# A mixture-of-experts stage: the shared expert's way down, one batch behind its way up

## The chip, the core and the metric

The kernel runs on one core of a Trainium2 chip. A core has TensorE (matrix products; PE in the profile), VectorE (DVE), ScalarE (ACT), GpSimd (POOL) and SyncE (SP, which here only issues DMAs). Each engine works through its own queue in order. Engines wait for each other, and for DMAs, through semaphores. Tiles lie in SBUF, 128 partitions wide; the results of TensorE go to tiles in PSUM, here each in a buffer of its own that is called a bank below.

The metric is the device time of one execution, in microseconds. The kernel before takes 3576.08 us (median of three runs, 3575.98 to 3579.71).

## The reference

The program is two layers, each a cross attention and a feed-forward part, over x of 4 batches of 512 tokens of 512 values. The change lies in the first layer's feed-forward part, a mixture of experts:

```python
scores = softmax(xf @ gate_w)                    # 8 experts
_, sel = top_k(scores + expert_bias, 2)
top_scores = take_along_axis(scores, sel, axis=1)
...
routed_in = xf[token_idx] * top_scores_sorted[:, None]
h = silu(ragged_dot(routed_in, w1, counts)) * ragged_dot(routed_in, w3, counts)
routed_out = ragged_dot(h, w2, counts)
out = silu(xf @ sw1) * (xf @ sw3) @ sw2          # the shared expert
out = out.at[token_idx].add(routed_out)
```

`xf` is the layer-normed x, and `out` is scaled by a gate and added to x. The hidden width is 448. Every token goes through the shared expert (`sw1`, `sw3`, `sw2`), and through two of eight routed ones.

## The kernel before

The program runs through four stages: int8 cross attention, this mixture of experts (`moe`), a second cross attention and a second feed-forward part. All arithmetic named here is f32; an f32 matmul or transpose of the program is two rows in the profile.

**Order.** The kernel is written with the Tile framework. It traces the calls, and a scheduler then decides in which order each engine's queue takes them, by the order of the calls and by when it takes the inputs to be ready; it also inserts all waits. A call that is wrapped by `Ordered` (lines 559 to 567) is pinned: it stays behind the call that was traced just before it on the same engine. In `moe` before the change nothing up to the slot loop is pinned. Tiles of one tag share a fixed number of buffers, and are given out in the order of the calls.

**First part of `moe`** (lines 660 to 679). For each batch b of four: a layernorm on VectorE (`k.layernorm`) makes `xn[b]` of four token tiles; sixteen transposes on TensorE (L670), four to each PSUM tile `pt` of the pool `ps_m` (two banks), which `k.evac` copies to `xT[b]`, by turns on VectorE (L120) and ScalarE (L122); then sixteen matmuls with the gate's weights (L675) into `pg`, also of `ps_m`, copied to the logits.

**Shared expert**, `shared(b)` (lines 683 to 705). The way up has four chunks m of 112 hidden columns. A chunk has four matmuls into `pu` and four into `pw` (L691; pool `ps_h`, four banks), a SiLU on ScalarE (L695) into `h`, and a product of `h` with `pw` on VectorE (L696). The way down has four token tiles t. A tile has four matmuls, one for each chunk of `h` (L700, pool `ps_o`, two banks), and a sum into the residual x on VectorE (L705). `shared(b)` does the four chunks, then the four tiles; it is called for all batches after the routing (L821).

**Routing** (lines 716 to 802). VectorE works out each token's two experts; two matmuls with the 0/1 matrix `both` count tokens (L750, L751); VectorE turns the counts into a row number of each token and choice, and into the owner of each of 39 slots of 128 rows.

**Scatters** (lines 807 to 819). For each of 16 token tiles and both choices, VectorE scales a tile of `xn` into `row` (tag `m_row`, four buffers, L811), and POOL issues an indirect DMA that writes it to `slots_in` in DRAM (L815).

**Slots** (lines 825 to 938). `load(s)` and `load_down(s)` bring the weights of slot s from its owner expert (L833: 1792 KB, L855: 896 KB, SP's queue) into `w13[s % 2]` and `w2[s % 2]`; `w13[1]` and `w2[1]` hold the shared expert's weights until slot 1. `load_rows(s)` (L837, ScalarE's queue) reads the slot's rows; it waits for all scatters. `turn_in(s)` transposes them (L861), `up(s)` and `down(s)` are the expert (L870, L888). The loop over s also calls, a few at a time, the steps of `split` (each loads a piece of a later stage's weights into one of two `raw` buffers, scales and centres it on VectorE at L1115 to L1137, casts it on ScalarE at L1141, subtracts on POOL at L1142, and stores it at L1143) and of `ternary` (weight sums at L1897 over pieces `t_raw`, which take the buffers of `xT` when these come free; codes at L1920). The scheduler takes such steps forward when it holds an engine to be free: the trace has them from 629 us on, in the midst of the shared expert.

After the loop, from L947 on, everything is pinned.

Of the kernel before, what the change touches and what calls it, by code (L numbers as in the profile page):

```python
# [11 lines left out]
F32 = mybir.dt.float32  # L12
# [6 lines left out]
ALU = mybir.AluOpType  # L19
# [578 lines left out]
def moe(k, split, codes8, scratch, ffn):  # L598
# [12 lines left out]
    with ExitStack() as ctx:  # L611
# [50 lines left out]
        for b in range(B):  # L662
            xn.append(p6.tile([P, TB, D], F32, tag="m_big", name=f"m_xn{b}"))
            xT.append(codes8.place(b, F32, f"m_xT{b}"))
        for b in range(B):
            k.layernorm([(xn[b][:, t, :], k.x[:, b * TB + t, :]) for t in range(TB)])
            for c in range(KC):
                pt = ps_m.tile([P, S], F32, tag="ps_m")
                for t in range(TB):
                    nc.tensor.transpose(pt[:, ts(t, P)], xn[b][:, t, ts(c, P)], k.ident)  # L670
                k.evac(xT[b][:, c, :], pt)
            pg = ps_m.tile([P, TB, E], F32, tag="ps_m")
            for t in range(TB):
                for c in range(KC):
                    nc.tensor.matmul(  # L675
                        pg[:, t, :], lhsT=xT[b][:, c, ts(t, P)], rhs=gw[:, c, :],
                        start=(c == 0), stop=(c == KC - 1),
                    )
            k.evac(lg[:, ts(b, TB), :], pg)

        silus = []

        def shared(b):

            h = p6.tile([HC, NHC, S], F32, tag="m_big", name=f"m_h{b}")
            for m in range(NHC):
                pu = ps_h.tile([HC, S], F32, tag="ps_h")
                pw = ps_h.tile([HC, S], F32, tag="ps_h")
                for half, pp in enumerate((pu, pw)):
                    for c in range(KC):  # L690
                        nc.tensor.matmul(  # L691
                            pp, lhsT=w13[1][:, c, half, ts(m, HC)], rhs=xT[b][:, c, :],
                            start=(c == 0), stop=(c == KC - 1),
                        )
                silus.append(nc.scalar.activation(h[:, m, :], pu, AF.Silu).ins)  # L695
                nc.vector.tensor_tensor(h[:, m, :], h[:, m, :], pw, ALU.mult)  # L696
            for t in range(TB):
                po = ps_o.tile([P, D], F32, tag="ps_o")
                for m in range(NHC):
                    nc.tensor.matmul(  # L700
                        po, lhsT=h[:, m, ts(t, P)], rhs=w2[1][:, m, :],
                        start=(m == 0), stop=(m == NHC - 1),
                    )
                xt = k.x[:, b * TB + t, :]
                nc.vector.scalar_tensor_tensor(xt, po, k.tg[:, 2:3], xt, ALU.mult, ALU.add)  # L705

        def bc(col):
            return col[:, :, None].to_broadcast([P, NT, E])
# [38 lines left out]


        pt = ps_m.tile([P, 2, NT, E], F32, tag="ps_m", name="r_counts")
        nc.tensor.matmul(pt[:, 0], lhsT=k.ones, rhs=both, start=True, stop=True)  # L750
        nc.tensor.matmul(pt[:, 1], lhsT=before, rhs=both, start=True, stop=True)  # L751
        nc.vector.tensor_copy(csum[0][:, 8:, :], pt[:, 0])
        src = 0
        for d in (1, 2, 4, 8):
# [63 lines left out]
                tc.declare_no_dep(scatters[-1], group="scatter", reason="rows are distinct")  # L818
                tc.add_to_no_dep_group("scatter", scatters[-1])

        for b in range(B):  # L821
            shared(b)
        got = {}

        def load(s):


            e = got["e", s] = nc.values_load(
                owners[:, s : s + 1], engines=(mybir.EngineType.SP,), min_val=0, max_val=E - 1,
                skip_runtime_bounds_check_because="it is at most E - 1 by construction",  # L830
            )
            got["new", s] = None if s < 2 else e != got["e", s - 2]
            nc.sync.dma_start(w13[s % 2], a["w13"][e], cond=got["new", s])  # L833
# [20 lines left out]
        def load_down(s):  # L854
            nc.sync.dma_start(w2[s % 2], a["w2"][got["e", s]], cond=got["new", s])  # L855

        def turn_in(s):
            work = got["work", s]
            pt = ps_m.tile([P, KC, P], F32, tag="ps_m")
            for c in range(KC):  # L860
                nc.tensor.transpose(pt[:, c, :], work[:, 0, ts(c, P)], k.ident)  # L861
            k.evac(work[:, 1, :].rearrange("p (c t) -> p c t", c=KC), pt)

        def up(s):
            work, w = got["work", s], w13[s % 2]
# [42 lines left out]
        ternary = ffn.weights(codes8, ps_o)  # L908
        for s in range(4):
            load_rows(s)  # L910
        for s in range(2):
            load(s)
            load_down(s)
        turn_in(0)
        up(0)
        turn_in(1)
        for s in range(SLOTS):
            if s + 1 < SLOTS:
# [1113 lines left out]
```

## Time and profile before

| what | value |
|---|---|
| median of three runs | 3576.08 us |
| the profiled execution, its own time | 3574.1 us |
| its span, first to last instruction | 3572.4 us |
| mean granted TensorE clock | 0.97 |
| `moe` from the first transpose to slot 0's first matmul | 629.88 to 870.42 us |
| shared expert's ways up, L691 | 256 rows, 642.8 to 845.6 us (starts) |
| shared expert's ways down, L700 | 128 rows, 689.2 to 868.7 us (starts) |
| slot loop's ways up, L870 | 312 rows for each of pu and pw, 870.4 to 1306.3 us (starts) |
| product on VectorE, L696 | 16 of 0.68 us |
| sum on VectorE, L705 | 16 of 0.74 us |
| row scaling, L811 / scatter, L815 | 32 of 0.485 us / 32 of 0.963 us |

A time in the table is read from the span's start. In lists of waits, a row says which instruction waited for which, the sum in us, how often, and the longest. In a timeline, a row gives start, length, engine, line, operation, output<-input, shape and count, and in brackets the idle time before it with what ended it. The granted clock is the share of TensorE's full clock that the chip allowed it.

### The profile page before, as it was taken

Reading aid. Unit: us, or ns where it says so; the run is one execution under the profiler, and the core shown is the slowest. Engines: PE = TensorE matmul, PEld = TensorE weight load, DVE = VectorE, ACT = ScalarE, POOL = GpSimd, SP = SyncE. Lnnn points to the kernel's source line nnn. Section 1 sums busy time; section 2 is a strip of 40 time slices with the busy share of each in tenths; the row PEclk is TensorE's granted clock in tenths of the full one; section 3 lists DMA queues with packets and bytes.
Section 4 is the critical chain, followed back from the end, with each engine's and each line's share of the span. In section 5 each row is a group of like instructions: output and inputs, shape, how many; then the busy total and the mean of one; then the engine's idle time right before and its main releaser. Section 6 shows DMA issues by size and latency. Waiting matters only on the chain.

```text
span 3572.4 us, 47015 instructions
## 1 busy us (share of the span) xinstructions
PE 3333.4 (93%) x15536; PEld 2190.3 (61%) x15552; DVE 2172.4 (61%) x4580; ACT 1544.1 (43%) x4456; POOL 1355.3 (38%) x1526
## 2 busy tenths in 40 slices
PE   6988987889999889989999999999999999999997
PEld 3544544534554444447777777776777777777775
DVE  6676767543133336525558766678766687676657
ACT  2544545111211223345554455554555554555543
POOL 1000000341000134624446654557545466544443
PEclk8999999899999999989999999999999999999998
DMA  5534441476354673552323233223332332333211
GB/s 183 156 98 130 121 101 41 167 254 234 104 198 151 225 257 128 177 174 72 115 98 107 101 115 110 95 99 108 109 125 92 118 107 77 128 105 111 83 60 36
DMA packets 223026, 452.86 MB, mean 127 GB/s; under 512 B 21440, under 2 KB 80320, under 8 KB 220224
## 3 DMA queue, kind: packets, MB, share of 16 engines
q1 hardware_dynamic: 206432, 412.62, 35.2%
q10 hardware_dynamic: 11232, 20.45, 1.7%
q0 software_dynamic: 5120, 16.78, 1.4%
q8 instruction: 125, 2.05, 0.2%
q14 instruction: 117, 0.96, 0.1%
HBM read 420.87 MB, written 116.98 MB: 151 GB/s over the span
## 4 chain that ended last, share of the span: by engine, by line
PE 73%; DVE 13%; DMA 4%; ACT 4%; POOL 3%; issue 3%; SPq 0%; DVEq 0%; POOLq 0%; ACTq 0%
PE ps_w L567 10%; PE pss L567 10%; PE ps_p L567 9%; PE ps_o L567 9%; PE ps_t L567 7%; PE m_pk L567 5%; PE po L888 3%; PE pu L870 3%; PE pw L870 3%; PE po L468 3%; PE pt L460 3%; DVE f_y L567 2%; PE pss L438 2%; PE pk L403 2%; PE pv L373 2%
## 5 line engine op out<-in xcount | busy, mean ns | idle before, releaser
L567 PEld LDWEIGHTS ps_w<-g_pT,g_v 128*128 128x128 f32 x2048 | 388.8, 191 | 299.7 <-issue 223.1
L567 ACT ACTIVATE g_p<-pss,nm 128x512 f32<-128x512 f32 x512 | 350.9, 685 | 479.7 <-DVE nm L567 436.4
L567 PE MATMUL ps_w<-g_pT,g_v 128*128 128x256 f32 x2048 | 530.4, 382 | 24.1 <-DVE f_y L567 13.7
L567 PE MATMUL pss<-g_kT,g_qT 128*128 128x512 f32 x1024 | 524.1, 594 | 0.9 <-ACT g_p L567 0.9
L567 POOL TENSOR_SCALAR g_p<-g_p,rs 128x512 f32<-128x512 f32 x512 | 368.4, 721 | 382.1 <-DVE rs L567 370.6
L567 DVE TENSOR_REDUCE nm<-pss 128x1 f32<-128x512 f32 x512 | 350.9, 685 | 102.7 <-PE pss L567 101.7
L567 PE MATMUL ps_t<-ident,g_p 128*128 128x128 f32 x2048 | 307.5, 273 | 0.0
L1142 POOL TENSOR_TENSOR hl<-raw,hl 128x512 fp32r<-128x512 f32 x80 | 102.0, 1282 | 519.2 <-ACT hl L1141 503.1
L567 POOL TENSOR_TENSOR g_rstd<-ss,neghalf 128x4 f32<-128x4 f32 (+1 forms) x192 | 185.0, 964 | 297.5 <-ACT ss L567 297.3
L567 PE MATMUL ps_p<-g_wq,g_xq 128*128 128x512 f32 x1024 | 282.3, 417 | 5.3 <-DMA g_wq<-s_q 4.9
L567 PE MATMUL ps_o<-g_wp,g_cq 128*128 128x512 f32 x1024 | 287.0, 423 | 0.0
L567 DVE COPY g_pT<-ps_t 128x512 f32<-128x512 f32 x244 | 167.1, 685 | 165.8 <-PE ps_t L567 165.4
L567 POOL TENSOR_TENSOR f_t<-f_y,f_c 128x512 f32<-128x512 bf16 (+1 forms) x180 | 206.6, 1148 | 155.4 <-DVE f_c L567 87.1
L567 PEld LDWEIGHTS ps_t<-ident,g_p 128*128 128x128 f32 x2048 | 243.8, 141 | 26.3 <-POOL g_p L567 1.1
L567 ACT COPY g_pT<-ps_t 128x512 f32<-128x512 f32 x268 | 156.1, 583 | 233.4 <-PE ps_t L567 233.4
L446 ACT ACTIVATE p<-pss,nm 128x512 f32<-128x512 f32 x256 | 175.3, 690 | 135.9 <-DVE nm L443 134.5
L567 PE MATMUL m_pk<-m_wx,m_ctxT 128*128 128x512 f32 x512 | 230.0, 592 | 0.0
L567 PEld LDWEIGHTS ps_o<-g_wp,g_cq 128*128 128x128 f32 x1024 | 196.7, 192 | 41.4
L567 PEld LDWEIGHTS ps_p<-g_wq,g_xq 128*128 128x128 f32 x1024 | 191.4, 190 | 48.9 <-issue 7.1
L443 DVE TENSOR_REDUCE nm<-pss 128x1 f32<-128x512 f32 x256 | 173.2, 687 | 70.7 <-PE pss L438 69.3
L567 ACT ACTIVATE junk<-ps_p 128x128 f32<-128x128 f32 x640 | 177.1, 277 | 68.5 <-PE ps_p L567 54.2
L567 DVE RECIPROCAL rs<-g_sm 128x1 f32<-128x1 f32 x512 | 82.5, 161 | 203.3 <-ACT g_p L567 201.4
(317 smaller groups left out, 6025.4 us busy)
## 6 DMA issues: line engine op xcount, KB each, us to landing
m_w<-in_w_dram SPq DMA_DIRECT2D x39, 1792.0 KB
g_wp<-s_proj SPq DMA_DIRECT2D x128, 512.0 KB
m_w<-in_w_dram SPq DMA_DIRECT2D x39, 896.0 KB
g_wq<-s_q SPq DMA_DIRECT2D x128, 256.0 KB
g_wq<-s_qx SPq DMA_DIRECT2D x128, 256.0 KB
st_k<-dhl_k SPq DMA_DIRECT2D x64, 256.0 KB
st_q<-dhl_q SPq DMA_DIRECT2D x64, 256.0 KB
s_proj<-hl SPq DMA_DIRECT2D x32, 512.0 KB
```

Of the source, the lines that this page charges most:

```text
L373: nc.tensor.matmul(pv, lhsT=ctxT[:, ic, ts(t, P)], rhs=wkvT[:, ic, D : 2 * D], start=(ic == 0), stop=(ic == KC - 1),)
L403: nc.tensor.matmul(pk, lhsT=wkvT[:, ic, ts(oc, P)], rhs=ctxT[:, ic, :], start=(ic == 0), stop=(ic == KC - 1),)
L438: nc.tensor.matmul(pss, lhsT=qk["q"][:, h, ts(qt, P)], rhs=qk["k"][:, h, :], start=True, stop=True,)
L443: nc.vector.tensor_reduce(nm, pss, AX.X, ALU.max, negate=True)
L446: nc.scalar.activation(p, pss, AF.Exp, bias=nm, accum_out=sums[:, qt, n : n + 1])
L460: nc.tensor.transpose(pt[:, c, :], p[:, ts(c, P)], k.ident)
L468: nc.tensor.matmul(po[ts(h, DH0)], lhsT=v[:, c, ts(oc * 4 + h, DH0)], rhs=pTs[h][:, c, :], start=(c == 0), stop=(c == TB - 1),)
L567: return lambda *args, **kw: self.tc.keep_in_program_order(call(*args, **kw))
L870: nc.tensor.matmul(pp, lhsT=work[:, 1, ts(c, P)], rhs=w[:, c, half, :], start=(c == 0), stop=(c == KC - 1),)
L888: nc.tensor.matmul(po, lhsT=work[:HC, 3, ts(m, P)], rhs=w[:, m, :], start=(m == 0), stop=(m == NHC - 1),)
L1142: nc.gpsimd.tensor_tensor(hl[:, 1, :], raw, hl[:, 0, :].bitcast(F32), ALU.subtract)
```

## The change

- All TensorE calls of `moe` before the slots, and the shared expert's last ways down, go through `TE = Ordered(tc, nc.tensor)`.
- The first part is cut into `turn(b)` (layernorm, transposes) and `gate(b)`. `turn(0)` comes first; then, for each b, `turn(b + 1)`, `gate(b)` and chunk b of batch 0's way up.
- `shared` is cut into `shared_up(b, m)`, one chunk, and `shared_down(b, t)`, one tile. `shared_up(1, 0)` and `shared_down(0, 0)` are called just ahead of the two counting matmuls. After the scatters, for b = 1, 2, 3 and each m, `shared_up(b, m)` is followed by `shared_down(b - 1, m)`.
- The last batch's four ways down come after `up(0)` of the slots. `load(1)` is called after `load_down(0)`, ahead of `turn_in(0)`, as before; `load_down(1)` is called after the last way down, and `turn_in(1)` after that.

```diff
-        for b in range(B):
+        TE = Ordered(tc, nc.tensor)
+        silus, hs = [], {}
+
+        def turn(b):
             k.layernorm([(xn[b][:, t, :], k.x[:, b * TB + t, :]) for t in range(TB)])
             for c in range(KC):
                 pt = ps_m.tile([P, S], F32, tag="ps_m")
                 for t in range(TB):
-                    nc.tensor.transpose(pt[:, ts(t, P)], xn[b][:, t, ts(c, P)], k.ident)
+                    TE.transpose(pt[:, ts(t, P)], xn[b][:, t, ts(c, P)], k.ident)
                 k.evac(xT[b][:, c, :], pt)
+
+        def gate(b):
             pg = ps_m.tile([P, TB, E], F32, tag="ps_m")
...
-        def shared(b):
-
-            h = p6.tile([HC, NHC, S], F32, tag="m_big", name=f"m_h{b}")
+        def shared_up(b, m):
+
+            if m == 0:
+                hs[b] = p6.tile([HC, NHC, S], F32, tag="m_big", name=f"m_h{b}")
+            h = hs[b]
+            pu = ps_h.tile([HC, S], F32, tag="ps_h")
+            pw = ps_h.tile([HC, S], F32, tag="ps_h")
+            for half, pp in enumerate((pu, pw)):
+                for c in range(KC):
+                    TE.matmul(
+                        pp, lhsT=w13[1][:, c, half, ts(m, HC)], rhs=xT[b][:, c, :],
+                        start=(c == 0), stop=(c == KC - 1),
+                    )
+            silus.append(nc.scalar.activation(h[:, m, :], pu, AF.Silu).ins)
+            nc.vector.tensor_tensor(h[:, m, :], h[:, m, :], pw, ALU.mult)
+
+        def shared_down(b, t):
+
+            po = ps_o.tile([P, D], F32, tag="ps_o")
             for m in range(NHC):
...
+                TE.matmul(
+                    po, lhsT=hs[b][:, m, ts(t, P)], rhs=w2[1][:, m, :],
+                    start=(m == 0), stop=(m == NHC - 1),
+                )
+            xt = k.x[:, b * TB + t, :]
+            nc.vector.scalar_tensor_tensor(xt, po, k.tg[:, 2:3], xt, ALU.mult, ALU.add)
+
+
+        turn(0)
+        for b in range(B):
+            if b + 1 < B:
+                turn(b + 1)
+            gate(b)
+            shared_up(0, b)
...
-        nc.tensor.matmul(pt[:, 0], lhsT=k.ones, rhs=both, start=True, stop=True)
-        nc.tensor.matmul(pt[:, 1], lhsT=before, rhs=both, start=True, stop=True)
+        shared_up(1, 0)
+        shared_down(0, 0)
+        TE.matmul(pt[:, 0], lhsT=k.ones, rhs=both, start=True, stop=True)
+        TE.matmul(pt[:, 1], lhsT=before, rhs=both, start=True, stop=True)
...
-        for b in range(B):
-            shared(b)
+
+        for b in range(1, B):
+            for m in range(NHC):
+                if (b, m) > (1, 0):
+                    shared_up(b, m)
+                    shared_down(b - 1, m)
...
-        for s in range(2):
-            load(s)
-            load_down(s)
+        load(0)
+        load_down(0)
+        load(1)
         turn_in(0)
         up(0)
+        for t in range(TB):
+            shared_down(B - 1, t)
+        load_down(1)
         turn_in(1)
```

More of the change, by code (lines that the diff above doesn't have):

```diff
@@ L674, in moe @@
                 for c in range(KC):
-                    nc.tensor.matmul(
+                    TE.matmul(
                         pg[:, t, :], lhsT=xT[b][:, c, ts(t, P)], rhs=gw[:, c, :],
@@ L679, in moe @@
             k.evac(lg[:, ts(b, TB), :], pg)
-        silus = []
-        def shared(b):
-            h = p6.tile([HC, NHC, S], F32, tag="m_big", name=f"m_h{b}")
-            for m in range(NHC):
[L687 to L705, printed above, removed]
@@ new lines, in shared_down @@
+        def shared_down(b, t):
+            po = ps_o.tile([P, D], F32, tag="ps_o")
+            for m in range(NHC):
+                TE.matmul(
+                    po, lhsT=hs[b][:, m, ts(t, P)], rhs=w2[1][:, m, :],
[9 more added lines that the diff above has]
+            shared_up(0, b)
```

## The prediction

> **What bounds the kernel now.** The page first: TensorE is busy nearly everywhere, so a change must be judged in its own stretch.
>
> ```profile
> span 3572.4 us, 47015 instructions
> PE 3333.4 (93%) x15536; PEld 2190.3 (61%) x15552; DVE 2172.4 (61%) x4580; ACT 1544.1 (43%) x4456; POOL 1355.3 (38%) x1526
> ```
>
> I then cut the mixture-of-experts part into stages: transposes, gate and first ways up; routing; the time in which the 32 row scatters are issued; the rest of the shared expert up to its last product; its last way down with the first two slots' ways up. The columns are length, busy time of the five engine rows, granted TensorE clock, DMA share, GB/s.
>
> ```profile
> 629.88:679.28 49.40, 48.57 (x234) 35.06 (x235) 28.92 (x65) 13.28 (x21) 6.25 (x5) 0.81 0.34 111
> 679.28:690.43 11.15, 11.15 (x29) 5.00 (x30) 10.98 (x37) 1.83 (x3) 2.63 (x3) 1.00 0.40 142
> 690.43:746.76 56.33, 42.83 (x89) 17.11 (x88) 30.71 (x59) 4.06 (x7) 37.00 (x35) 0.88 0.77 275
> 746.76:854.47 107.71, 94.21 (x205) 38.47 (x203) 46.12 (x87) 17.95 (x30) 26.69 (x23) 0.93 0.67 233
> 854.47:882.55 28.08, 27.11 (x66) 12.94 (x67) 10.17 (x13) 3.43 (x6) 4.98 (x4) 0.89 0.86 297
> ```
>
> TensorE is not full in the last three, and its clock is down. Its waits from 679 to 883 us:
>
> ```profile
> PE po L700 <- DVE m_h L696: 14.8, 5, 6.4
> PE po L700 <- DVE x_res L705: 8.0, 1, 8.0
> PE pw L691 <- DVE m_h L696: 4.9, 2, 2.5
> ```
>
> 27.7 us, all of it for VectorE, and most where a way down starts straight after the same batch's way up. The order of time shows a second price, a slow clock after each wait (16 rows take 6.87 us at full clock, 26 take 11.16):
>
> ```profile
> 705.10 9.77 PE L700 MATMUL po<-m_w,m_h 112*128 112x512 f32 x16 [7.99 <-DVE x_res L705]
> 734.55 5.26 PE L691 MATMUL pw<-m_xT,m_w 128*112 128x512 f32 x8 [2.50 <-DVE m_h L696]
> 855.20 14.11 PE L700 MATMUL po<-m_w,m_h 112*128 112x512 f32 x26 [6.41 <-DVE m_h L696]
> ```
>
> Eight undisturbed rows start 3.43 us apart (714.71 to 718.15), so one row is 0.429 us. From 679.80 to 869.14 TensorE issues 214 rows of ways up and 128 of ways down, 146.8 us of work in 189.3: **42.5 us lost**, 27.7 waiting and 14.8 slow. That is all the change can win there.
>
> But why is VectorE late? Its own waits from 690 to 855 us:
>
> ```profile
> DVE m_row L811 <- DMA slots_in<-m_row,r_posi: 25.0, 10, 7.5
> DVE raw L1137 <- DMA raw<-in_w_kv_dram: 15.4, 3, 6.2
> DVE raw L1137 <- DMA raw<-in_w_q_dram: 14.1, 2, 8.7
> DVE part_w_gu L1897 <- DMA t_raw<-in_w_gu_dram: 11.7, 3, 4.3
> DVE part_w_dn L1897 <- DMA t_raw<-in_w_dn_dram: 9.2, 2, 4.8
> DVE m_h L696 <- ACT m_h L695: 4.1, 2, 2.8
> DVE x_res L705 <- PE po L700: 4.0, 2, 2.2
> ```
>
> It waits 77.9 us for DMAs (with 2.5 in a row not shown) and 8.1 us for TensorE and ScalarE. So VectorE's queue, in which the shared expert's products and sums stand behind scatter rows, weight-splitting steps and weight sums that wait for their loads, **paces this stretch**. TensorE follows it. The chain of waits agrees: between 693 and 855 us it runs through scatters, raw loads and the POOL halves, with little TensorE.
>
> **What the change does, part by part.** up(b,m) is 16 rows, 6.9 us; down(b,t) is 8 rows, 3.4 us. No instruction is added or removed.
>
> *Order pinned, downs one batch behind.* down(b,0) no longer needs a product finished just before, and a product has until the up after the next (four banks) instead of 0 to 3.4 us: 3.4+6.9+3.4 = 13.7 us. That removes TensorE's reason for most waits. It does not make VectorE's queue shorter: the products h(b,m) are still in it, with the same 32 rows, splits and sums, and the framework chooses that queue's order, not the change. So I follow VectorE.
>
> *Counts later.* Before the counts matmul TensorE had issued 42 rows of up (to 679.28). Now it must issue 64, 16 of up(1,0) and 8 of down(0,0): 46 more, 19.7 us, counts at 699.0. The transposes stand in a fixed order on two banks. In the trace L691 rows fill the gaps while a bank is emptied (0.59 us on ScalarE, 0.69 on VectorE), and the only visible wait is 0.58 us. Bounds 0 to 6 us (four batches with some 1.5 each, worked out from these copies and 0.44 us for four warm transposes); I take 2, near the row: 701. The routing before it (gate's copy at 667.83 to 679.28, 11.4 us) now lies beside 17 us of TensorE work and is hidden.
>
> *Scatter rows.* First scatter 11.15 us after the counts: 712.2. In the queue before, from the first scatter to the last row TensorE was given four downs and two ups, 64 rows. The same 64 rows are now up(1,2), down(0,2), up(1,3), down(0,3), up(2,0). So h(2,0) comes where h(1,1) came, 744.94-690.43 = 54.5 us after the first scatter: 766.7. Scatters thus move some 22 us later on POOL; who needs them are the slots' row loads, issued after the first SiLU of batch 3 (822.2 before), with room.
>
> *To the last product.* From h(1,1) to h(3,3) (744.94 to 854.47) VectorE took 109.5 us for 224 TensorE rows (96.1 us): 1.139. Now 168 rows, 72.1 us, are left after up(2,0): 82.2 us, **h(3,3) at 848.9**. Without the 8.0 us in which VectorE waited for the others the ratio is 1.056, and it would be 842.8. I take the first; the queue's DMA waits stay.
>
> *The end of the stage.* Before, 28.1 us followed h(3,3). Now turn_in(0) and up(0) stand ahead of the last way down and lie beside the wait. With TensorE 8.3 us ahead of VectorE (846.2 against 854.47 before), the last up ends at 840.6; down(2,3) 3.4, turn_in(0) with its copy 1.6, up(0) 6.0: 851.6, so the last way down waits for nothing. Its 32 rows (13.7) and turn_in(1) with up(1) (7.5) end at 872.9 against 882.55: 9.6 us.
>
> *Loads.* load(1) needs up(3,3); its queue was 10 us late before (856.62 after 846.2). Now 24.8 us of TensorE work lies between, enough for the load. load_down(1) is called later and its wait for the last down can hold load(2), called behind it on SP: 0 (SP is given load(2) first) to 5 us (both transfers, 2.7 MB at the stretch's 297 GB/s take 9 us, up(2) comes some 11 us later, SP was up to 10 us late). I take 1, near the row: L870's waits for weights come to 10.8 us in eight places.
>
> Sum: 9.6 - 1, about 9 us. The slot loop behind it is TensorE's (869 to 1000: 128.75 of 130.9 busy), so it starts and ends earlier. Profiled execution 3574.1, so 3565; the median of the runs is 2.0 above it: **3567 us**.
>
> *A rule against the change.* The Trainium skill's page "TensorE: Matmul & The Clock Gate", section "A second HAM failure mode: psum-queue depth-cycling", says that cycling through PSUM banks with small idles between groups can let the clock swing between half and full. The change alternates two pools at every step. The 296 rows after the counts are 127 us; if half of them ran at half clock, that would be 64 us more. The row: from 642.80 to 679.80 TensorE alternated three pools, was busy 36.75 of 37.00 us, at clock 0.92: at most 11 us on 127, most of it beside VectorE's waits. I go by the row. The same page's Part 1 lets only an idle window of some 3.4 us cool the array, for about 3.4 us at half rate: three waits here, 5 us in all. The rows say 14.8, and the 2.50 us wait already cost 1.7.
>
> **The rivals.**
> 1. *TensorE paces.* If the queue's entries fall more loosely, every wait and slow clock goes: 42.5 less some 8 us for turns and loads, 3542. For it: 13.7 us of room against a lag of 0.5 to 8.4 us in 773 to 854. Against: 77.9 us of DMA waits. Chance 0.17.
> 2. *Slower: splits crowd the products.* Nothing pins VectorE, and products 10.3 us apart leave openings that the framework fills. In 746.76 to 854.47 it placed 21 steps, 5.1 us each. Two more ahead of h(3,3) eat the gain; from 3.2 on it is slower by over 0.2%; four give 9 - 20.5, so 3588. For it: 31 of the 80 casts on L1141 have begun by 854.5, so 49 steps are still to be had. Against: two raw buffers limit them. Chance 0.28.
> 3. *Given back.* What is won is lost in the slot loop to weight loads that come later (its waits are at 1221 to 1252 us): 3576. Chance 0.10.
> Forecast's own case: 0.45, from 3557 (ratio 1.056, no turn waits) to 3577 (6 us of turns, 5 of loads).
>
> **Numbers.** 0.2%, 7.2 us, is about what can be told from no change. Of the forecast's 0.45, 0.28 is a gain over that. Faster 0.28+0.17, same 0.17+0.10, slower 0.28. The range reaches down to half of rival 1 (3545) and up past rival 2's four steps (3590), leaving 0.18 out.
>
> **What would show it.** Counts near 701; h(2,0) near 767, after the last row; h(3,3) near 849 with VectorE's DMA waits still about 75 us; TensorE's waits for products at two or three places among the scatters; slot 1's way up ending near 873. Wrong if h(3,3) comes under 835 (rival 1) or past 858 (rival 2), or if slot 1 is early and the end is not.

## The result, and the profile after

The changed kernel takes 3585.94 us (median of 14 runs, 3580.71 to 3590.59), the kernel before 3576.34 us on the same chip (14 runs, 3571.24 to 3579.71). The ratio is 1.003, 95% interval [1.0022, 1.0038]: **9.6 us slower**, where 9 us faster was forecast. The profiled execution of after took 3589.61 us, 3.7 above its median; that of before lies 2.2 below its own.

The page of after first: nearly the same instructions, and each engine's busy time is within 4.1 us of before's, while the span is 15.5 us longer. No work was added.

```profile
span 3587.9 us, 47004 instructions
PE 3335.1 (93%) x15536; PEld 2192.1 (61%) x15552; DVE 2176.5 (61%) x4580; ACT 1543.5 (43%) x4456; POOL 1355.6 (38%) x1526
```

To find it, the span is cut at three marks: the first transpose of `moe`, slot 0's first way down, and the first row behind the slot loop. After comes to the first transpose 1.8 us later (631.7 against 629.9), ahead of anything that the change touches; the fourteen kernels below come there between 628.0 and 633.7. From the first transpose to slot 0's way down (**the stage**) after takes 258.4 us, before 254.0: +4.4. From there to the end of the loop (**the loop**) it takes 441.9 against 431.7: +10.2. The rest is 1.1 shorter. So there are two losses, not one. These 15.5 us are of one profile each; the medians differ by 9.6, so each of the two losses may be some us smaller than it is here.

The stage, cut as before was cut: first transpose to counts, to the first scatter, to the end of the scatters, to the last product h(3,3), to the end of slot 1's way up. Columns as there.

```profile
631.70:703.90 72.20, 70.52 (x280) 42.99 (x281) 36.13 (x79) 15.61 (x25) 8.77 (x7) 0.87 0.37 119
703.90:715.83 11.93, 11.93 (x32) 5.32 (x31) 11.66 (x37) 1.74 (x3) 2.54 (x2) 1.00 0.61 208
715.83:772.95 57.12, 46.20 (x103) 19.09 (x102) 30.73 (x59) 5.70 (x10) 37.69 (x37) 0.91 0.73 261
772.95:856.57 83.62, 62.57 (x144) 26.03 (x142) 34.38 (x58) 11.75 (x21) 20.58 (x16) 0.89 0.71 249
856.57:889.02 32.45, 28.94 (x66) 13.60 (x67) 14.82 (x26) 5.11 (x9) 7.60 (x6) 0.86 0.72 249
```

Up to the end of the scatters this goes as the forecast's plan. In the fourth stretch TensorE is idle for 21 of 83.6 us, and the last is longer than before's (32.45 against 28.08), where the forecast had 24.0 from h(3,3) to its end (848.9 to 872.9). TensorE's waits from the counts to slot 0's way down:

```profile
PE po L567 <- DVE m_h L700: 19.2, 2, 10.9
PE pu L890 <- ACT m_work L122: 15.4, 1, 15.4
PE pu L567 <- ACT m_h L699: 0.9, 1, 0.9
```

The waits for sums and for products ahead of a way up, 12.9 us before, are gone. The waits for products ahead of a way down have not gone: they are fewer and longer (19.2 us in two, 14.8 in five before). The first, 10.9 us, is down(1,0)'s for h(1,3): TensorE gave it 13 us after up(1,3), and the product ended 24 us after it, at 755.75. A new row of 15.4 us has come: slot 0's way up (L890) waits for ScalarE's copy of its transposes (L122). TensorE's order of time shows where (start, length, and in brackets the idle time before it):

```profile
840.20 3.60 PE L567 MATMUL po<-m_w,m_h 112*128 112x512 f32 x8
843.64 1.04 PE L881 MATMUL pt<-ident,m_work 128*128 128x128 f32 x8
860.08 1.86 PE L890 MATMUL pu<-m_w,m_work 128*128 128x448 f32 x2 [15.40 <-ACT m_work L122]
861.73 1.70 PE L890 MATMUL pw<-m_w,m_work 128*128 128x448 f32 x2
...
866.09 0.92 PE L890 MATMUL pu<-m_w,m_work 128*128 128x448 f32 x2
...
869.10 13.90 PE L567 MATMUL po<-m_w,m_h 112*128 112x512 f32 x32
```

Both turns, `turn_in(0)` and `turn_in(1)`, were done at 844.7 (an f32 transpose is one row in these profiles, only a matmul is two, so the eight rows are four transposes for each). The copy that up(0) waits for begins only at 859.45. What stood ahead of it is in the same stretch of the timeline, ScalarE's rows:

```profile
845.54 0.62 ACT L1164 CAST hl<-raw 128x512 fp32r<-128x512 f32 x1 [8.69 <-DVE m L1139]
...
846.87 0.59 ACT L699 ACTIVATE m_h<-pu 112x512 f32<-112x512 f32 x1
...
856.40 0.62 ACT L1164 CAST hl<-raw 128x512 fp32r<-128x512 f32 x1 [8.94 <-DVE raw L1140]
...
858.92 0.62 ACT L1164 CAST hl<-raw 128x512 fp32r<-128x512 f32 x1 [1.90 <-DVE raw L1140]
...
859.45 0.58 ACT L122 COPY m_work<-pt 128x512 f32<-128x512 f32 x1
```

ScalarE did nothing from 847.5 to 856.4: the next instruction of its queue was a cast (L1164) of a splitting step, which waits for VectorE's part of that step (L1160 to L1140). VectorE's part waited for a load, in the same stretch:

```profile
853.89 0.61 DVE L1160 TENSOR_SCALAR raw<-raw,pcol_sb 128x256 f32<-128x256 f32 x2 [6.96 <-DMA raw<-in_w_kv_dram]
```

ScalarE's waits from 713 to 870 us say the same over the whole stretch:

```profile
ACT hl L1164 <- DVE raw L1140: 79.8, 11, 20.3
ACT hl L1164 <- DMA raw<-in_w_proj_dram: 29.5, 6, 9.5
ACT hl L1164 <- DMA m_work<-slots_in: 9.7, 1, 9.7
```

A queue that stood at casts for 119 of 157 us (sum of the three rows) is no place for a copy that TensorE is to wait for. VectorE's waits for DMAs from 713 to 860 us are much as before: 67.8 us in the rows below and 2.2 in one not shown, in 147 us, against 77.9 in 165:

```profile
DVE m_row L827 <- DMA slots_in<-m_row,r_posi: 24.6, 14, 6.9
DVE raw L1160 <- DMA raw<-in_w_q_dram: 19.5, 2, 13.1
DVE part_w_dn L1920 <- DMA t_raw<-in_w_dn_dram: 10.2, 2, 7.1
DVE raw L1160 <- DMA raw<-in_w_kv_dram: 7.4, 2, 7.0
DVE raw L1160 <- DMA raw<-in_w_qx_dram: 6.1, 2, 5.6
```

The loop's 10.2 us have another place. Counted from slot 0's way down, slot 26's way up begins after 267.2 us in before and 267.9 in after, slot 27's after 279.0 and 287.1: most of the loss, 7.4 us, lies between these two. At the loop's end it is 10.2. The rest of the loop from slot 22 on, in before and in after, with the columns of the stages:

```profile
1120.20:1315.50 195.30, 172.79 (x498) 83.81 (x496) 71.46 (x131) 45.15 (x78) 38.71 (x31) 0.98 0.64 224
```

```profile
1126.50:1332.00 205.50, 177.71 (x496) 86.53 (x497) 75.70 (x135) 45.72 (x78) 40.45 (x31) 0.95 0.60 214
```

In both TensorE is idle for 22 to 28 us and its clock is down, and in after by more: half of the difference is idle time, half are slow rows. The dearest place in after is slot 26, here with slot 27's rows behind it, in TensorE's order of time:

```profile
1168.22 1.10 PE L901 MATMUL pt<-ident,m_work 128*112 128x128 f32 x4 [4.04 <-DVE m_work L895]
...
1170.89 6.51 PE L908 MATMUL po<-m_w,m_work 112*128 112x512 f32 x8 [0.71 <-ACT m_work L122]
...
1184.20 0.65 PE L901 MATMUL pt<-ident,m_work 128*112 128x128 f32 x4 [0.78 <-DVE m_work L895]
...
1185.53 3.70 PE L908 MATMUL po<-m_w,m_work 112*128 112x512 f32 x8 [0.24 <-ACT m_work L122]
```

The slot's product (L895) came 4.04 us late from VectorE, and the way down behind it took 6.51 us in place of 3.70, slow rows after the wait: 6.9 us in one slot. VectorE's rows show what the product stood behind. Its second input was done at 1164.2, but a splitting step was ahead of it in the queue, and that step waited for its load:

```profile
1165.44 0.62 DVE L1160 TENSOR_SCALAR raw<-raw,pcol_sb 128x256 f32<-128x256 f32 x2 [4.31 <-DMA raw<-in_w_kv_dram]
...
1167.56 0.61 DVE L895 TENSOR_TENSOR m_work<-m_work,pw 128x448 f32<-128x448 f32 x1
```

So it is what happened to the copy in the stage, with a product and VectorE's queue. Before has no wait for a product over 0.8 us in slots 22 to 26; its list of waits there:

```profile
PE po L888 <- ACT m_work L122: 2.7, 4, 1.4
PE pt L881 <- DVE m_work L875: 1.6, 2, 0.8
```

So there were two questions. Is the copy the stage's loss, and what else bounds the stage? And what makes the loop longer, whose calls the change doesn't touch?

### The profile page after: what moved, and what is told of

It is laid out like the page before. It is cut to its first block, busy times and chain, and to the rows that moved or that the text cites. A ratio compares the mean times of both kernels' runs of the same rounds, so it can differ in the third digit from the quotient of the medians.

```text
span 3587.9 us, 47004 instructions
## 1 busy us (share of the span) xinstructions
PE 3335.1 (93%) x15536; PEld 2192.1 (61%) x15552; DVE 2176.5 (61%) x4580; ACT 1543.5 (43%) x4456; POOL 1355.6 (38%) x1526
## 4 chain that ended last, share of the span: by engine, by line
PE 73%; DVE 13%; DMA 4%; ACT 3%; POOL 3%; issue 3%; SPq 0%; DVEq 0%; POOLq 0%; ACTq 0%
PE ps_w L567 10%; PE pss L567 10%; PE ps_p L567 9%; PE ps_o L567 9%; PE ps_t L567 7%; PE m_pk L567 5%; PE po L908 3%; PE pu L890 3%; PE pw L890 3%; PE po L468 3%; PE pt L460 3%; DVE f_y L567 2%; PE pss L438 2%; PE pk L403 2%; PE pv L373 1%
## 5 line engine op out<-in xcount | busy, mean ns | idle before, releaser
L567 PEld LDWEIGHTS ps_w<-g_pT,g_v 128*128 128x128 f32 x2048 | 388.9, 191 | 299.8 <-issue 223.3
L443 DVE TENSOR_REDUCE nm<-pss 128x1 f32<-128x512 f32 x256 | 173.2, 688 | 72.2 <-PE pss L438 70.5
```

What stands on the lines that cost most here:

```text
L443: nc.vector.tensor_reduce(nm, pss, AX.X, ALU.max, negate=True)
L567: return lambda *args, **kw: self.tc.keep_in_program_order(call(*args, **kw))
```

## The experiments

The table has all of them, by the marks above. "Left" is how many splitting steps had not begun their cast when slot 0's way down began; the three columns in us and the count are from one profile each, the ratio is to the kernel before, with its 95% interval.

| kernel | stage | h(3,3) from first transpose | loop | left | ratio |
|---|---|---|---|---|---|
| before | 254.0 | 224.6 | 431.7 | 45 | 1 |
| after | 258.4 | 224.8 | 441.9 | 46 | 1.003 [1.0022, 1.0038] |
| last downs ahead of slot 0 | 256.1 | 224.9 | 440.2 | 47 | 1.0021 [1.0012, 1.003] |
| turn_in(0) early | 252.5 | 225.2 | 442.9 | 46 | 1.0016 [1.0009, 1.0023] |
| after, steps held back | 223.3 | 191.7 | 500.2 | 76 | 1.0083 [1.0069, 1.0097] |
| before, steps held back | 222.1 | 193.2 | 501.3 | 76 | 1.0105 [1.0087, 1.0123] |
| counts first | 259.6 | 229.4 | 442.6 | 46 | 1.0039 [1.0026, 1.0053] |
| old head, new tail | 255.4 | 223.8 | 434.4 | 43 | 1.0003 [0.9994, 1.0011] |
| new head, old tail | 260.4 | 230.8 | 442.5 | 47 | 1.0042 [1.0028, 1.0056] |
| after, two steps left out | 252.2 | 217.9 | 433.1 | 43 | 0.9995 [0.9987, 1.0004] |
| old head, new tail, both turns early | 253.0 | 221.5 | 433.3 | 43 | 1.0 [0.9991, 1.0008] |
| after, both turns early | 249.3 | 224.4 | 440.1 | 46 | 1.0006 [0.9998, 1.0015] |
| before, two steps twice | 257.8 | 228.9 | 442.0 | 47 | 1.0029 [1.002, 1.0037] |
| both turns early, codes sooner | 262.4 | 229.4 | 434.5 | 43 | 1.0015 [1.0009, 1.0022] |

Stage and loop, taken together against before, come out 1.6 to 5.5 us above the difference of the medians in ten of the thirteen rows, 8.2 in "after, steps held back", and at or under it in two: each row is one profile, and before's lies 2.2 us below its median. A difference of 2 us between two rows is not read as anything.

### Is it the copy? Two orders of the tail

The first takes the last ways down back ahead of slot 0, so that TensorE does not stand before up(0).

```diff
         load(1)
+        for t in range(TB):
+            shared_down(B - 1, t)
+        load_down(1)
         turn_in(0)
         up(0)
-        for t in range(TB):
-            shared_down(B - 1, t)
-        load_down(1)
         turn_in(1)
```

> One part of the change undone: the last batch's four ways down are called ahead of turn_in(0) and up(0) again. Theory Q (the copy of turn_in(0) to up(0) stands in ScalarE's queue behind split steps, 15.4 us of TensorE waiting, so calling up(0) first hides nothing): the last way down waits for h(3,3) near 857 instead, up(0) follows it without a wait, and slot 0's way down starts at about 886, some 4 us earlier than in the changed kernel (890.1): about 3582 against 3586. Rival H (the loss comes from the head, where the counts are 24.6 us later): the stage ends as late as in the changed kernel or later, since up(0) lies behind again: 3586 to 3592.

The stage came to 256.1, 2.3 us shorter, little more than can be read. The 15.4 us are gone, but the last ways down now wait for h(3,3), 12.0 us at their longest. So the change's new tail gains nothing by its order: TensorE waits at the one place or at the other.

The second leaves the change's order and puts `turn_in(0)` one chunk earlier, so that its copy stands ahead of the last splitting steps in ScalarE's queue:

```diff
-                if (b, m) > (1, 0):
+                if (1, 0) < (b, m) < (B - 1, NHC - 1):
...
-        load(1)
         turn_in(0)
+        shared_up(B - 1, NHC - 1)
+        shared_down(B - 2, NHC - 1)
+        load(1)
         up(0)
```

> The changed kernel, with turn_in(0) called one step earlier, ahead of up(3,3), and with the slots' first row loads called ahead of that. Theory Q: the copy then stands ahead of the split steps that surround h(3,3); up(0) starts right after down(2,3), near 845 instead of 860, beside VectorE's delay; the last way down still waits for h(3,3) near 857, slot 0's way down starts near 879, 11 us earlier than in the changed kernel: about 3575, if the slot loop takes as long. Rival H: h(3,3) is what ends late and up(0) in front of it is worth little, 0 to 3 us: 3583 to 3586.

TensorE's waits of this kernel from 700 to 892 us:

```profile
PE po L567 <- DVE m_h L700: 19.9, 2, 12.0
PE pu L890 <- ACT m_work L122: 2.9, 1, 2.9
...
PE pu L890 <- issue: 2.4, 1, 2.4
```

The copy's wait falls from 15.4 to 2.9 us, and the stage from 258.4 to 252.5, under before. up(0) now begins at 843.8 (the forecast had it at 845.6), and the last way down waits for h(3,3), as the 12.0 shows. The copy is a cause: 5.9 us by the profiles, 5.2 by the medians, each against its own runs of before. The loop stayed at 442.9, so the time came to 3580.50 where about 3575 was expected.

Later `turn_in(1)` went early as well. In the run above TensorE still stood 2.4 us between its transposes and slot 1's way up (the row marked issue):

```diff
         turn_in(0)
+        turn_in(1)
         shared_up(B - 1, NHC - 1)
...
-        turn_in(1)
```

> The changed kernel with both turn_in calls ahead of up(3,3), so e2 with turn_in(1) early too. Theory Q: stage 3 to 6 us shorter than e2's 252.5, 247 to 250. Theory S: still 34 steps ahead or fewer, loop 440 to 443: about 3576. Rival: if the loop's extra is not the head's, it falls to 432 here too: 3567.

```profile
PE po L567 <- DVE m_h L700: 18.9, 2, 10.4
PE pu L890 <- ACT m_work L122: 3.5, 1, 3.5
```

The first two rows of this kernel's waits, from 703 to 893 us; the 2.4 us are gone, and the stage is 249.3: 9.1 us shorter than after and 4.7 shorter than before. This is the gain that the change's order has once its copies are not behind casts. Ratio 1.0006 [0.9998, 1.0015]: the loop takes it back.

### What paces the stage? The steps held back

In after and in before, every load of a splitting step or a weight sum is kept behind the issue of load(1). `NoSync` and `SCHED_ONLY` make this a rule for the scheduler's order alone; no wait is added to the program.

```diff
-        nc.sync.dma_start(raw, of)
+        k.held(nc.sync.dma_start(raw, of))
...
+    def held(self, sent):
+        self.tc.add_manual_dep(
+            sent.ins, self.behind.name,
+            mybir.DependencyInfo(
+                mybir.DependencyClass.NoSync, mybir.DependencyReason.SCHED_ONLY
+            ),
+            reason="not needed early",
+        )
```

> The changed kernel with all loads of the weight-splitting steps and of the weight sums held behind load(1) on SP, so that neither stands in VectorE's and ScalarE's queues before h(3,3). Theory Q: TensorE waits only among the scatter rows (about 11 us), h(3,3) follows up(3,3) within 2 us, slot 0's way down starts 25 to 30 us earlier than in the changed kernel (near 862); the slot loop is longer, since it has 80 steps instead of some 46; total open, 3560 to 3600. Rival H (the head and the scatters' later start hold the stage): slot 0's way down starts no more than 10 us earlier.

> The kernel before, with all loads of splits and weight sums held behind load(1) as in e3. Tells whether the queue of VectorE also paced the stage of the kernel before, and what the change's order is worth by itself when that is gone. Theory Q: from the first transposes to slot 0's way down takes 254.0 us in the kernel before and 223.3 in e3; here TensorE waits only for the scatter rows and for the product ahead of each first way down (2 to 3 us each), so 225 to 240; the loop as long as in e3, about 500. Rival (the kernel before's stage is TensorE's own waits for its own order, not the queue): over 248 us.

The stage falls to 223.3 and 222.1: by 35.1 and 31.9 us, and to the same in both orders. The stage of held after, first transpose to slot 0's way down, in one row, and TensorE's waits:

```profile
630.80:854.10 223.30, 215.20 (x628) 103.24 (x629) 79.89 (x162) 23.51 (x38) 37.10 (x37) 0.95 0.30 111
```

```profile
PE po L576 <- issue: 3.7, 2, 2.8
PE pw L576 <- issue: 2.2, 1, 2.2
PE po L919 <- ACT m_work L131: 2.0, 3, 1.5
```

TensorE is busy for 215 of 223 us, and no wait for a product is left (held before has one, of 6.8 us). VectorE's busy time in the stage is 79.9 us; the same stretch of after has 128.5 (631.7 to 890.1). So it is the steps and weight sums in the queues of VectorE and ScalarE that pace the stage, as forecast, and not TensorE's order: without them the stages of the two orders differ by 1.2 us. That the held loads also leave the DMA engines freer (111 GB/s against 214) is a rival, but the scatters show no gain from it: VectorE waits 23.1 us for them here and 24.6 in after. The loop then grows by 58 and 70 us, because 30 and 31 steps more are left to it: **1.9 to 2.2 us a step**. In the stage they cost 1.0 to 1.2 us each (35.1 over the 30 that left it, 31.9 over 31). Both prices include the weight sums that were held with the steps, and the first rests on a profile that lies 7.2 us above its kernel's median. Over the whole run held after takes 3605.69 us, more than the 3560 to 3600 that were expected, and held before 3614.09 (two runs only): 8.4 us apart, with intervals that overlap, so whether the order is worth something once the steps are gone stays open.

### Head or tail?

If the later counts (703.9 against 679.3) and with them the later scatters are what costs, then taking the two extra calls from ahead of the counts must shorten the stage:

```diff
-        shared_up(1, 0)
-        shared_down(0, 0)
...
-                if (b, m) > (1, 0):
-                    shared_up(b, m)
-                    shared_down(b - 1, m)
+                shared_up(b, m)
+                shared_down(b - 1, m)
```

> The changed kernel with up(1,0) and down(0,0) called after the two counting matmuls instead of ahead of them: counts and scatters 10.3 us earlier, no other edit. Theory Q: VectorE has the same entries up to h(3,3), so the end of the stage moves by 0 to 4 us, slot 0's way down 886 to 890: 3582 to 3586; if the routing on VectorE is not done at that point TensorE waits up to 6 us for it. Rival H: all that follows the scatters comes 10 us earlier, slot 0's way down near 880: 3576.

The counts came 6.0 us earlier, from the first transpose, not 10.3, since TensorE waited 4.1 us for the routing; the stage took 259.6, no shorter, and the time, 3589.61, was over both expectations. The copy's wait stood again, at 18.1 us. So 6 us of later scatters are not the cause; the next run takes off all of the 22.8.

Then the two halves of the change, each alone. Old head: transposes, gate and first ways up in the scheduler's order, and the pinned alternation from batch 1 on.

```diff
-        turn(0)
+        pinned, TE = TE, nc.tensor
         for b in range(B):
-            if b + 1 < B:
-                turn(b + 1)
+            turn(b)
             gate(b)
-            shared_up(0, b)
...
-        shared_up(1, 0)
-        shared_down(0, 0)
...
+        for m in range(NHC):
+            shared_up(0, m)
+        TE = pinned
         for b in range(1, B):
             for m in range(NHC):
-                if (b, m) > (1, 0):
-                    shared_up(b, m)
-                    shared_down(b - 1, m)
+                shared_up(b, m)
+                shared_down(b - 1, m)
```

> The change's tail with the head of the kernel before: transposes, gate, batch 0's ways up and the counts unpinned as before, counts near 679; ways up of batches 1 to 3 with the ways down one batch behind; last ways down after up(0). Theory Q: VectorE still has to work through the same entries after the counts, 20 us earlier; TensorE has 24 rows more to do after the counts; h(3,3) 0 to 6 us earlier than in the changed kernel, up(0) still waits 10 us or more for turn_in(0)'s copy: stage 252 to 259 us (258.4 in the changed kernel). Rival H: stage 235 to 245, since the scatters are 25 us earlier. The loop is read apart: 432 (before) or 440 to 443 (changed).

Old tail: the change's head, then for each batch its four ways up and its four ways down, and slot 0 behind them.

```diff
+        for t in range(1, TB):
+            shared_down(0, t)
         for b in range(1, B):
             for m in range(NHC):
                 if (b, m) > (1, 0):
                     shared_up(b, m)
-                    shared_down(b - 1, m)
+            for t in range(TB):
+                shared_down(b, t)
...
-        load(0)
-        load_down(0)
-        load(1)
+        for s in range(2):
+            load(s)
+            load_down(s)
         turn_in(0)
         up(0)
-        for t in range(TB):
-            shared_down(B - 1, t)
-        load_down(1)
```

> The change's head with the tail of the kernel before: ways down straight behind the same batch's ways up, all of them ahead of slot 0. Theory Q: the new tail is worth little, since VectorE paces; here TensorE waits at every first way down and the last ways down follow h(3,3): stage 256 to 266 us (258.4 in the changed kernel). Rival H: stage about 275, the kernel before's 254 and the 20 us by which the counts come later.

Stages: neither 254.0, head alone 260.4, tail alone 255.4, both 258.4. The head alone costs 6.4 us in the stage, far from the 20 by which its counts come later. The tail alone costs 1.4, too little to be read, the copy's wait included, which comes with the tail whatever the head is (TensorE's waits of old head with new tail):

```profile
PE pu L888 <- ACT m_work L122: 16.2, 1, 16.2
```

The loop divides the kernels more clearly: 434.4 with the old head, 442.5 with the new one. **The loop's loss comes with the head**, nearly 200 us ahead of it. What differs at the loop's start is how much of the other work is done: 43 steps left with the old head, 46 or 47 with the new one. Whether that number is what counts is the next question.

The old head was run again with both turns ahead of shared_up(3,3), as the diff above has it:

> The head of the kernel before, the change's tail, and turn_in(0) and turn_in(1) called ahead of up(3,3). Theory Q: without the copy's wait (16.2 us in e6) up(0) lies beside the wait for h(3,3), and turn_in(1)'s copy does not delay up(1) (some 5 us in e2): stage 255.4 - 9 = 244 to 249 us. Theory S: with as many steps done ahead as in e6 (37) the loop takes 432 to 436. Both together: about 3569, 0.2% under the kernel before. Rival L (the loop's length goes its own way with any edit of the order): loop 440 or more, 3578.

Stage 253.0 and loop 433.3, ratio 1.0 [0.9991, 1.0008]. The loop is as expected, but the stage is 4 us over its 244 to 249: with this head TensorE still waits 8.1 us for the copy, and 10.4 for sums. So this is not yet the tail without its copy's wait, and what came of it can't be told from no change.

### Is it the number of steps left?

Two of the 80 splitting steps are left out of after: two pieces of w_q of the second attention are copied unsplit to where their halves belong, so that what is computed from them differs.

```diff
+    for c in range(2):
+        for half in range(2):
+            nc.sync.dma_start(s["q"][0, :, c, half, :], a["w_q"][0, :, c, :])
...
     for i in range(NP):
         for name in ("q", "qx"):
-            steps += [partial(query, name, i, c) for c in range(KC)]
+            left_out = 2 if (i, name) == (0, "q") else 0
+            steps += [partial(query, name, i, c) for c in range(left_out, KC)]
```

> The changed kernel with two of the 80 splitting steps left out: the pieces 0 and 1 of the first query weight are copied unscaled, uncentred and unsplit from DRAM to DRAM at the start. Asks what the slot loop's extra 8 to 11 us (441.9 in the changed kernel, 431.7 before) are. Theory S (one step fewer done ahead makes the loop reach its two steps a slot one slot sooner, at 1.1 us a slot and a stall of 4 us where two loads stand ahead of a product): with two steps fewer the loop takes 431 to 436. Rival (the slot loop's order of its own, whatever the count): 438 to 443. The stage before it: one to two steps fewer ahead of h(3,3), 0 to 11 us shorter, or the same if the scheduler takes the next ones forward.

And before, with the first two steps done twice:

```diff
-    steps = []
+    steps = [partial(query, "q", 0, c) for c in range(2)]
     for i in range(NP):
```

> The kernel before with 82 splitting steps: the first two are done twice, with the same result. Theory S (what counts is how many steps are left at slot 0: 45 in the kernel before, 46 in the changed one): 47 are left, the loop takes 440 to 445 and the kernel 8 to 13 us longer, 3584 to 3589; the stage may take up to 5 us more. Rival L: loop 432 to 436, as the order of TensorE is that of the kernel before: 3577 to 3580.

The loop of after falls from 441.9 to 433.1; that of before rises from 431.7 to 442.0. Two steps are 4 us at the price found above; here they are 8.8 and 10.3. And the place is the same: with two steps more, before's slot 26 has its way up begin 2.2 us later than in before, and slot 27 9.4 us later, with this in TensorE's order of time:

```profile
1166.98 1.05 PE L881 MATMUL pt<-ident,m_work 128*112 128x128 f32 x4 [4.47 <-DVE m_work L875]
...
1169.65 5.80 PE L888 MATMUL po<-m_w,m_work 112*128 112x512 f32 x8 [0.76 <-ACT m_work L122]
```

These are after's two rows over again, in a kernel without a line of the change. The traces of all twelve kernels of the table that don't hold steps back agree. With 46 or 47 steps left, seven kernels, there is one wait for a product of 3.8 to 4.5 us in slot 26, each time behind a step that had waited 4.1 to 5.1 us for a piece of w_kv; with its slow rows it costs 6.3 to 7.0 us. With 43 to 45 left, five kernels, no such wait is over 0.8 us there. From slot 26's way up to slot 27's it is 18.7 to 19.4 us in the seven and 11.3 to 14.7 in the five, and the whole loop is 440.1 to 442.9 in the seven and 431.7 to 434.5 in the five.

Counting casts by slot, from one way down to the next, shows the shift. All kernels do 10 to 13 steps in slots 0 to 21, and about two a slot from slot 28 on; between, a few slots take more. Slots 22 to 27 have 0, 2, 0, 4, 1, 3 steps in six of the seven (0, 2, 1, 3, 1, 3 in the other). Before has 0, 1, 2, 0, 4, 1, the crowded slot **one slot later**, and after with two steps left out has 0, 0, 2, 2, 1, 3, with no slot of four.

That the loop goes with the number left is shown by adding and by taking away, in kernels of either head. That it acts through one step that comes ahead of slot 26's product is read from the rows: no run moved that step alone, and some 3 us of the 8.8 to 10.3 lie elsewhere in the loop.

The run with two steps left out says something of the stage too. It took 252.2 us with the copy's wait still in it, at 16.2 us, because h(3,3) came 7 us earlier (217.9). So the stage's length has two terms, the copy and h(3,3), and the second moves by as much with the steps that the scheduler places.

Last, the codes out of the crowd's way: after with both turns early, and two ternary pieces handed out in a slot in place of one.

```diff
-            if ternary:
-                ternary.pop(0)()
+            for _ in range(2):
+                if ternary:
+                    ternary.pop(0)()
```

> The kernel after with turn_in(0) and turn_in(1) both ahead of shared_up(3,3), as in the run with both turns early, and two ternary pieces handed out per slot in place of one, so that the ternary codes are done by about slot 13, before the loop comes to its two split steps a slot. Theory (the loop's extra at slots 22 to 26 is split steps and codes falling in the same slots, one slot sooner where one or two more steps are left): the stage stays at 249 us (246 to 252), the loop falls from 440.1 to 425 to 434 us though 46 steps are left at slot 0, and the time is 3565 to 3573 us, under the kernel before by 0.1 to 0.3%. Rival (the codes' loads and work crowd the early slots as much as they did the late ones, or the extra comes from the number of steps alone, whatever stands beside them): the loop stays at 439 us or more and the time at 3576 to 3583 us.

This one doesn't decide it. The last codes were done in slot 14 in place of 27, and from slot 26's way up to slot 27's it took 11.3 us in place of 18.7, as the theory wanted; but by slot 16's way up the loop was 9.9 us behind the run it is compared with, and by slot 23's still 3.8. And the scheduler, given other calls behind, placed the stage's steps anew: 37 begun before slot 0 in place of 34, a stage of 262.4 where 246 to 252 was expected, and 43 steps left, with which the other kernels have a loop of this length (433.1 to 434.4) with the codes where they were. So nothing here shows that the codes matter. It shows at least how much the scheduler's placing can move the stage: 13 us between two kernels whose calls up to slot 0 are the same. No version that computes the same is measurably faster than the kernel before.

## Why the prediction was wrong

**What bounds the stage: right.** VectorE's queue, with the steps in it, paces: with the steps held back the stage is 32 and 35 us shorter.

**Counts, scatters, h(2,0): right.** Taken from the first transpose, the counts came at 72.2 us (forecast 71.1), the first scatter 11.9 later (11.15), h(2,0) 54.9 behind it (54.5), after the last row as forecast. The 2 us for the turns and the hidden routing came out about as they were put (1.1 us over in sum). TensorE's waits for products were put at two or three places among the scatters; there were two in all, one there (10.9 us) and one behind (8.3).

**"h(3,3) at 848.9": 7.7 us too early.** 1.8 of it is the run's later start, 2.2 come from the steps above, and 3.7 are the ratio 1.139: it gave 82.2 us from h(2,0), and 85.9 were measured. From the first transpose h(3,3) stands where it stood before, 224.8 against 224.6, with two steps fewer done ahead of it (29 against 31). Why the queue took no less time for them is open; two kernels with equal calls differ by 5 us there.

**"turn_in(0) with its copy 1.6": this is the step that failed.** TensorE needed 1.0 us for both turns and then 15.4 us for the copy. The last way down was to start at 851.6 and started at 869.1. Of these 17.5 us, 5.7 are h(3,3) itself, which ended at 857.3 (1.8 of them the run's later start); the other 11.8 are the copy and the slow rows of up(0) after it (first groups 1.86 and 1.70 us in place of 0.92). The forecast had followed VectorE's queue and what stands in it, and then priced a copy on ScalarE, whose queue holds the other half of the same steps, by its own length. With the turns early the stage came to 4.7 us under before, half of the 9.6 forecast; the other half is h(3,3), 224.4 from the first transpose where 219.0 was forecast.

**"Slot loop behind it is TensorE's, so it starts and ends earlier": failed too, by as much.** Its length was carried over unchanged, read from 869 to 1000 us, where TensorE is busy nearly all the time. It is not TensorE's from slot 22 on: 22.5 us idle there before, at a clock of 0.98. Two steps more in before, and two fewer in after, move it by 10.3 and 8.8 us. The change leaves it one step more than before (46 against 45). All seven kernels with 46 or more have the late product of slot 26 and none of the others has; no run moved the number by one alone.

**The rivals.** "TensorE paces" fell with h(3,3). "Splits crowd the products" had the sign and nearly the size (3588), by a mechanism that did not act: fewer steps, not more, went ahead of h(3,3), and the crowding was on ScalarE's queue ahead of a copy, and in the loop. "Given back" had a place in the loop right but not its cause: waits for weights in slots 22 and later are 6.0 us in after against 5.1 before; one of 4.3 lies behind slot 27's way up, where after loses 2.1 us in all, and what is lost there varies from kernel to kernel. The forecast's 10.8 us of waits for weights in eight places counted each wait twice, for the weight load and for the matmul behind it: TensorE's own are 4.3 us in four for L870's `pu` rows from 876 to 1320 us.

**The clock rule.** The granted clock over the stage is 0.89 in after and 0.90 in before, so alternating the pools brought it down by no more than 0.01; the row was right to go by. The forecast's estimate from the Trainium skill's page "TensorE: Matmul & The Clock Gate", section "A second HAM failure mode: psum-queue depth-cycling", was 64 us, and by the row at most 11. Part 1 of that page has the array go to half rate after an idle window of about 3.4 us, and back after about as long a busy one, by estimate 1.7 us of lost work a time. Here the 15.4 us idle cost 3.1 (the first four groups of up(0) against 0.92 each) and the 4.04 us cost 2.8, both more than that estimate; the waits of 1.9 us in the last section, shorter than that window, cost 1.7.

## What to carry to other kernels

Before a step is moved, find the queue of every instruction it needs, copies out of PSUM included, and price it by what stands at the head of that queue at that moment; a copy of 0.6 us made TensorE wait 15.4. Where a scheduler fills idle engines with other work, ask of any change how much of that work it leaves for later, and what a unit of it costs there: about 2 us here, and 4 to 5 where it put a step's load ahead of a product. And a later stretch is "bound by TensorE" only where the rows say so to its end.

## What the runs showed of the hardware

The slow clock after a wait doesn't go by the wait's length alone. After 1.90 us (after with both turns early, last ways down) eight rows took 5.40 us in place of 3.70; after 2.44 us (`turn_in(0)` early, slot 1's way up) the first group took 0.99 and the next 0.92, full speed; after 1.54 us (two steps left out, slot 26's way down) eight rows took 3.70. What else decides isn't shown by these runs.

```profile
861.90 3.70 PE L567 MATMUL po<-m_w,m_h 112*128 112x512 f32 x8 [0.58 <-DVE x_res L711]
867.49 5.40 PE L567 MATMUL po<-m_w,m_h 112*128 112x512 f32 x8 [1.90 <-DVE x_res L711]
872.73 0.92 PE L890 MATMUL pu<-m_w,m_work 128*128 128x448 f32 x2
```

Those rows are from the first of the three, in TensorE's order of time. So in these runs a wait of 1.9 us cost 3.6 in all, itself and 1.7 of slow rows, and one of 2.4 little more than itself.
